# Attention with a separate maximum pass: chunks of 512 keys instead of 400 in that pass, and the last 66 keys of four query tiles in one chunk

## The chip, the cores and the metric

The kernel runs on one core of a Trainium2 chip. A core has a matrix engine (TensorE, PE in the profile; its weight loads are PEld), a vector engine (VectorE, DVE), a scalar engine (ScalarE, ACT), GpSimd (POOL), and a queue engine (SyncE, SP) that here only starts transfers. Each engine works through its own list of instructions in order and waits for the others by semaphores. The metric is the device time of one launch in microseconds (us). Matrix results go to PSUM, a small memory from which ACT and DVE read; a PSUM tile of this kernel is 128 partitions by two banks of 512 fp32 numbers.

## The reference

One layer of cross-attention and a feed-forward block over x (2048 rows of 256), with a context of 1601 keys of width 192, all in fp32:

```python
x = x + xattn(layernorm(x), ctx, mask, ...)
x = x + ffn(layernorm(x), k0, k1, k2, s0, s1, s2)

# xattn: 16 heads of 64
q, k, v = layer_norm(x) * g @ Wq, *split(ctx @ Wkv)
k, v = [null_k; k], [null_v; v]              # 1602 keys
attn = softmax(where(mask, q @ k.T / 8, -max))
out = layer_norm((attn @ v) @ Wout) * g_out
# ffn: three matrices of +1 and -1, relu between
```

The softmax needs a maximum over the 1602 keys for each query and head before the exponentials.

## The kernel before

The 16 heads are worked in 8 pairs p, the 2048 queries in 4 blocks b of 512: 32 units (p, b), written out in this order (`units`, L427), with the instructions of each engine in the order of the program (a manual schedule; no planner moves anything). A head of a pair lies on one half of the 128 partitions, so that matmuls for the two heads (j = 0, 1) use two halves of the array.

Scores are made twice. The exact pass (`exps`, L343) makes them in fp32 with the keys on the partitions, in 13 key tiles of 128 (the last has 66), two PSUM buffers in turn; for k < 2 a further matmul (L366) subtracts the maximum, and later tiles add the difference of the keys to what already lies in the buffer. ACT makes the exponentials (L368) into the tiles e, and POOL adds these up into acc (L556, L558), from which the denominator comes. The maximum pass (`max_chunk`, L310) makes the same scores in the rounded type fp32r, with the queries on the partitions: for each of the 4 query tiles t of a block the 1602 keys in 4 chunks (`CHUNKS`: 402, 400, 400, 400), each a pair of matmuls into a PSUM tile of its own and one DVE reduction (L321) over it. Unit u does the exact pass of its own block and, between the key tiles, the maximum pass of the next unit: 16 chunks behind 13 key tiles, two of them behind tiles 0, 4 and 8 (`extra`). `max_combined` (L323) takes the maximum over the four chunks.

After the key tiles PE runs the weighted sums (`weighted`, L375) for all 13 tiles, with the denominator of the unit before among them (`divided`, L390), then turns the maxima (`max_turned`, L328), projects the unit before's output (`project_out`), the queries of the unit after the next (`project_q`), and a part of the next pair's keys or values (`project_k`, `project_v`).

PSUM has two pools of two tiles: `spare` (the two score buffers, the weighted sum, the output projection) and `flex` (the chunks of the maximum pass, the denominator, the turned maxima, the other projections). A tile of a pool is free again when its reader is done. The last unit has no next one, and so no maximum pass.

Before the loop the first unit is prepared by hand (L478 to L518). There `CHUNKS` also sets how the context is loaded (L439) and how the first pair's keys are made (`first_keys`, L204), and the PSUM tiles come from both pools in turn (`slot`). Keys of the other pairs have a division of their own (L221). After the loop comes the feed-forward block (from L628), which the change doesn't touch.

Of the kernel before, what the change touches and what calls it, by code (L numbers as in the profile page):

```python
# [13 lines left out]
ALU = mybir.AluOpType  # L14
AX = mybir.AxisListType
# [5 lines left out]
KEYS = M + 1  # L21
CD = 192
HEADS, DH = 16, 64
# [3 lines left out]
NB = N // 512  # L27
KC = (KEYS + 127) // 128
KLAST = KEYS - 128 * (KC - 1)
CHUNKS = ((0, 402), (402, 400), (802, 400), (1202, 400))  # L30
EPS = 1e-5
MASKED = -3.0e38

# [2 lines left out]
def xattn_ffn(ctx, tc, x, ctxT, mask, g_norm, null_kv, wq, wkv, wout, g_out, k0, k1, k2, s0, s1, s2, out):  # L36
    nc = tc.nc
# [11 lines left out]
    def spare(name):  # L49
        return ps_s.tile([128, 2, 512], F32, tag="s", name=name)  # L50
# [92 lines left out]
    with ExitStack() as att:  # L143
# [40 lines left out]
        pairs, queries = {}, {}  # L184
# [19 lines left out]
        def first_keys(n, get):  # L204

            kT, _, kr = pairs[0]
            start, w = CHUNKS[n]
            keys = ds(start, w)
            ps = get(f"psk_0_{n}")
            nc.tensor.matmul(ps[:, 0, :w], weights[0][1][:, 0, :], ctx_a[:, keys], start=True, stop=False)  # L210
            nc.tensor.matmul(ps[:, 0, :w], weights[0][2][:, 0, :], ctx_b[:, keys], start=False, stop=True)

            nc.vector.tensor_tensor(kT[:, keys], ps[:, 0, :w], keep[:, keys], ALU.mult)
            nc.vector.scalar_tensor_tensor(kr[:, keys], drop[:, keys], nullk[:, 0:1], kT[:, keys], ALU.mult, ALU.add)
            if n == 0:
                nc.vector.tensor_copy(kT[:, 0:1], nullk)
# [25 lines left out]
        def keys_stepped(p):  # L242

            kT = pairs[p][0]
            for at in range(256 * ((KEYS - 1) // 256), 0, -256):
                w = min(256, KEYS - at)
                nc.gpsimd.tensor_tensor(kT[:, ds(at, w)], kT[:, ds(at, w)], kT[:, ds(at - 256, w)], ALU.subtract)  # L247

        def first_values(n, get):

            v = pairs[0][1]
            tiles = range(4 * n, min(4 * n + 4, KC))
            rows = 128 if n < 3 else KLAST
            ps = get(f"psv_0_{n}")
            for i, t in enumerate(tiles):
                keys = ds(128 * t, rows)
                out_t = ps[:rows, 0, ts(i, 128)]
                nc.tensor.matmul(out_t, ctx_a[:, keys], weights[0][1][:, 1, :], start=True, stop=False)
                nc.tensor.matmul(out_t, ctx_b[:, keys], weights[0][2][:, 1, :], start=False, stop=True)
            w = len(tiles)  # L260
            nc.scalar.copy(
                v[:rows, ds(4 * n, w), :], ps[:rows, 0, : 128 * w].rearrange("p (t d) -> p t d", d=128)
            )
            if n == 0:
                nc.vector.tensor_copy(v[0:1, 0, :], nullv)
# [42 lines left out]
        maxima, shifts = {}, {}  # L308

        def max_chunk(p, b, n, get=flex):  # L310
            t, c = divmod(n, 4)
            if n == 0:
                maxima[p, b] = wp.tile([128, 4, 2, 4], F32, tag="mx", name=f"mx_{p}_{b}")
            start, w = CHUNKS[c]
            ps = get(f"max_{p}_{b}_{n}")
            for j in range(2):
                rows = ts(j, DH)
                nc.tensor.matmul(  # L318
                    ps[:, j, :w], queries[p, b][1][rows, ts(t, 128)], pairs[p][2][rows, ds(start, w)], start=True, stop=True
                )  # L320
            nc.vector.tensor_reduce(maxima[p, b][:, t, :, c], ps[:, :, :w], AX.X, ALU.max)  # L321

        def max_combined(p, b):  # L323

            cols = mcol.rearrange("p (j c) -> p c j", j=2)[:, 0:4, :]
            nc.vector.tensor_reduce(cols, maxima[p, b], AX.X, ALU.max, negate=True)
# [13 lines left out]
        def rows_of(k):  # L340
            return 128 if k < KC - 1 else KLAST

        def exps(p, b, k, sT):  # L343

            kT, qT, mT = pairs[p][0], queries[p, b][0], shifts[p, b]  # L350
            n = rows_of(k)
            ps = sT[k % 2]
            for j in range(2):
                rows = ts(j, DH)
                nc.tensor.matmul(  # L355
                    ps[:n, j, :],
                    kT[rows, ds(128 * k, n)],
                    qT[rows, :],
                    start=k < 2,
                    stop=k >= 2,  # L360
                    skip_group_check=k >= 2,
                )
            if k < 2:
                for j in range(2):
                    rows = ts(j, DH)
                    nc.tensor.matmul(ps[:n, j, :], ones_r[rows, :n], mT[rows, :], start=False, stop=True)  # L366
            e = ep.tile([128, 2, 512], F32, tag="e", name=f"e_{p}_{b}_{k}")
            nc.scalar.activation(e[:n], ps[:n], AF.Exp, bias=maskb[:n, k : k + 1])  # L368
            return e
# [46 lines left out]
        def input_turned(b, get=flex):  # L416
            pt = get(f"xT_{b}")
            for j in range(4):
                for c in range(2):
                    nc.tensor.transpose(pt[:, c, ts(j, 128)], y_sb[:, 4 * b + j, ts(c, 128)], ident)  # L420
            nc.scalar.mul(xnT[:, b, 0, :], pt[:, 0, :], gn_sb[:, 0:1])
            if b == 1:
                nc.scalar.mul(xnT[:, b, 1, :], pt[:, 1, :], gn_sb[:, 1:2])
            else:
                nc.vector.tensor_scalar_mul(xnT[:, b, 1, :], pt[:, 1, :], gn_sb[:, 1:2])  # L425

        units = [(p, b) for p in range(NP) for b in range(NB)]  # L427
        extra = {0, 4, 8}

        begin = tc.manual_schedule()  # L430
        begin.__enter__()
# [1 line left out]
        def load_x(b):  # L433
            nc.sync.dma_start(out=x_sb[:, ts(b, 4), :], in_=x[ts(b, 512), :].rearrange("(c p) d -> p c d", p=128))

        load_pair(0)
        for b in range(1, NB):
            load_x(b)
        for n, (at, w) in enumerate(CHUNKS):  # L439
            skip = 1 if n == 0 else 0  # L440
# [45 lines left out]
        first_keys(1, slot)  # L486
        project_q(0, 0, slot)
        for t in range(4):
            max_chunk(0, 0, 4 * t, slot)
            if t == 1:  # L490
                first_keys(2, slot)
        for t in range(4):
            max_chunk(0, 0, 4 * t + 1, slot)
            if t == 1:
                first_keys(3, slot)
                keys_stepped(0)
# [6 lines left out]
        nc.vector.tensor_scalar(  # L503
            maskb[:KLAST, KC - 1 : KC], mcol_u8[:KLAST, KC - 1 : KC], -MASKED, MASKED, ALU.mult, ALU.add
        )
        for n in (2, 3):
            for t in range(4):
                max_chunk(0, 0, 4 * t + n, slot)
                if n == 2 or t == 3:
                    if t % 2 == 1:  # L510
                        first_values((0, 1)[t // 2] if n == 2 else 2, slot)
                if n == 3 and t == 1:
                    input_turned(1, slot)
        max_combined(0, 0)
        project_q(0, 1, slot)
        max_turned(0, 0)
# [3 lines left out]
        with tc.manual_schedule():  # L520
            for u, (p, b) in enumerate(units):
                nxt = units[u + 1] if u + 1 < len(units) else None
# [16 lines left out]
                    nc.gpsimd.tensor_tensor(y0, y0, gout_sb.unsqueeze(1).to_broadcast([128, 4, D]), ALU.mult)  # L539
                    nc.gpsimd.tensor_tensor(x0, x0, y0, ALU.add)  # L540

                es, n = [], 0
                acc = lp.tile([128, 2, 512], F32, tag="acc", name=f"acc_{p}_{b}")
                for k in range(KC):
                    if k == 0:

                        odd = spare(f"sT_{p}_{b}_1")
                        sT = [spare(f"sT_{p}_{b}_0"), odd]
                    es.append(exps(p, b, k, sT))
                    for _ in range(2 if k in extra else 1):  # L550
                        if nxt is not None:
                            max_chunk(*nxt, n)
                            n += 1
                    m = rows_of(k)
                    if k == 1:
                        nc.gpsimd.tensor_tensor(acc, es[0], es[1], ALU.add)  # L556
                    elif k > 1:
                        nc.gpsimd.tensor_tensor(acc[:m], acc[:m], es[k][:m], ALU.add)  # L558
# [199 lines left out]
```

## Time and profile before

| | |
|---|---|
| time, median of 3 runs | 1346.53 us (1346.41 to 1347.16) |
| the profiled execution | 1346.17 us, span 1344.1 us |
| granted TensorE clock | 0.994 |
| start, to the first scores of unit 0 | 48.5 us |
| 32 units | 48.5 to about 1155 us |
| feed-forward block | about 1155 us to the end |
| DVE reductions of the maximum pass (L321) | 512, 478.5 us busy, 987 ns each |
| PE matmuls of the maximum pass (L318) | 1024, 279.3 us busy |
| ACT exponentials (L368) | 416, 456.1 us busy, 1114 ns each |
| PE scores (L355) | 1664, 440.3 us busy |
| PE weighted sums (L375) | 1664, 369.5 us busy |

A group's "mean ns of one" is the time from its start to its end; instructions of one engine overlap, so that the distance from start to start, which the timeline gives, is shorter. An fp32 matmul appears as two passes, each with its own weight load, and a pair of heads as two rows of the same time. In the timeline the first column is the start, the second the length of the merged row, "xN" the instructions in it, and the brackets hold the idle time of the engine before it and who ended it.

### The profile page before, as it was taken

How to read it: one execution, taken by the hardware profiler on the slowest of the kernel's cores; microseconds unless marked ns; L12 is line 12 of the kernel's file. 1: busy time of each engine (PE TensorE's matmuls, PEld its weight loads, DVE VectorE, ACT ScalarE, POOL GpSimd, SP SyncE). 2: the span in 40 equal slices, each digit the busy share in tenths (PEclk: the TensorE clock that was granted, in tenths of full speed). 3: DMA queues.
4: the chain of work that ended last, by engine and by line, in shares of the span. 5: the costliest groups of instructions: out<-in, count | busy, mean ns of one | idle time of the engine just before them, and what ended most of it. 6: DMA issues, size and time to landing. Idle time of an engine off the chain costs nothing.

```text
span 1344.1 us, 16270 instructions
## 1 busy us (share of the span) xinstructions
PE 1304.6 (97%) x6528; PEld 654.8 (49%) x6528; DVE 845.8 (63%) x913; ACT 614.6 (46%) x676; POOL 1005.5 (75%) x508
## 2 busy tenths in 40 slices
PE   5989999999999999999999999999999999999998
PEld 2534444444444444444444444444444443688887
DVE  6777666666677566766666667666666784564431
ACT  1746444444444444445554555444444557421120
POOL 4468888898888888888888888888888999711100
PEclk9889999999999999999999999999999999999999
DMA  5000000000000000000000000000000010000000
GB/s 138 21 0 5 0 1 12 5 0 1 12 1 5 1 1 12 4 1 1 12 4 1 1 13 4 0 1 5 1 16 1 0 39 1 1 0 16 17 16 16
DMA packets 16092, 13.18 MB, mean 10 GB/s; under 512 B 2433, under 2 KB 15873, under 8 KB 16017
## 3 DMA queue, kind: packets, MB, share of 16 engines
q1 hardware_dynamic: 14640, 10.57, 2.8%
q10 hardware_dynamic: 896, 1.23, 0.3%
q8 instruction: 51, 0.84, 0.3%
q0 software_dynamic: 480, 0.34, 0.1%
q14 instruction: 25, 0.20, 0.0%
HBM read 10.04 MB, written 2.10 MB: 9 GB/s over the span
## 4 chain that ended last, share of the span: by engine, by line
PE 82%; ACT 8%; DVE 7%; issue 1%; DMA 1%; POOL 0%; SPq 0%; ACTq 0%; DVEq 0%
PE av L375 26%; PE sT L355 21%; PE ps L654 10%; PE max L318 6%; ACT e L368 6%; PE psq L199 4%; PE po L383 4%; DVE mx L321 4%; PE ps L677 2%; PE den L393 2%; PE psv L276 2%; PE psk L224 1%; DVE kr L236 1%; PE psv L288 1%; PE psk L229 1%
## 5 line engine op out<-in xcount | busy, mean ns | idle before, releaser
L558 POOL TENSOR_TENSOR acc<-acc,e 128x1024 f32<-128x1024 f32 (+1 forms) x352 | 849.4, 2413 | 27.6
L321 DVE TENSOR_REDUCE mx<-max 128x2 f32<-128x800 f32 (+1 forms) x512 | 478.5, 987 | 98.1 <-PE max L318 93.8
L368 ACT ACTIVATE e<-sT,maskb 128x1024 f32<-128x1024 f32 (+1 forms) x416 | 456.1, 1114 | 73.4 <-PE sT L355 44.7
L355 PE MATMUL sT<-qT,kT 64*128 64x512 f32 (+1 forms) x1664 | 440.3, 604 | 4.8 <-ACT e L368 1.3
L375 PE MATMUL av<-e,v 128*64 128x512 f32 (+1 forms) x1664 | 369.5, 594 | 0.8 <-ACT e L368 0.3
L318 PE MATMUL max<-kr,qr 64*128 64x400 f32 (+1 forms) x1024 | 279.3, 562 | 8.5 <-DVE mx L321 5.1
L375 PEld LDWEIGHTS av<-e,v 128*64 128x64 f32 (+1 forms) x1664 | 116.7, 137 | 237.8 <-issue 219.3
L318 PEld LDWEIGHTS max<-kr,qr 64*128 64x128 f32 x1024 | 97.6, 185 | 195.1 <-DVE mx L321 151.2
L355 PEld LDWEIGHTS sT<-qT,kT 64*128 64x128 f32 (+1 forms) x1664 | 139.7, 182 | 86.5 <-ACT e L368 75.5
L606 ACT COPY avs<-av 128x512 f32<-128x512 f32 x32 | 18.7, 585 | 324.0 <-PE av L375 324.0
L395 DVE RECIPROCAL aoT<-den 128x512 f32<-128x512 f32 x31 | 104.0, 3356 | 68.0 <-PE den L393 68.0
L556 POOL TENSOR_TENSOR acc<-e,e 128x1024 f32<-128x1024 f32 x32 | 77.5, 2421 | 86.2 <-ACT e L368 86.2
L333 DVE TENSOR_TENSOR mT<-mt,pick 128x512 fp32r<-128x512 f32 x32 | 22.1, 691 | 98.5 <-PE mt L331 98.5
L654 PE MATMUL ps<-h0hi,w 128*128 128x512 f32 x256 | 79.6, 392 | 0.0
L654 PE MATMUL ps<-h0lo,w 128*128 128x512 f32 x256 | 78.9, 389 | 0.0
L119 POOL TENSOR_TENSOR y_sb<-y_sb,gout_sb 128x256 f32<-128x256 f32 x12 | 9.3, 775 | 89.0 <-DVE y_sb L86 89.0
L200 ACT ACTIVATE qr<-psq 128x512 fp32r<-128x512 f32 x32 | 19.1, 597 | 100.4 <-PE psq L199 100.4
L199 PE MATMUL psq<-xnT,wq 128*128 128x512 f32 x128 | 62.1, 608 | 2.5 <-DVE xnT L425 2.5
L643 DVE SCALAR_TENSOR_TENSOR h1lo<-ps,h1hi 128x1024 fp32r<-128x1024 f32 x16 | 19.6, 1223 | 68.4 <-ACT h1hi L642 68.4
L383 PE MATMUL po<-wo,aoT 128*128 128x256 f32 x256 | 60.6, 380 | 0.0
L247 POOL TENSOR_TENSOR kT<-kT 128x256 f32<-128x256 f32 (+1 forms) x48 | 31.6, 659 | 38.3 <-DVE kr L236 22.1
L642 ACT ACTIVATE h1hi<-ps 128x1024 fp32r<-128x1024 f32 x16 | 16.4, 1025 | 94.6 <-PE ps L654 94.6
(147 smaller groups left out, 1025.6 us busy)
## 6 DMA issues: line engine op xcount, KB each, us to landing
x_sb<-in_x SPq DMA_DIRECT2D x4, 512.0 KB, 9.2
out_x<-o SPq DMA_DIRECT2D x8, 256.0 KB, 2.1
wa<-in_wkv SPq DMA_DIRECT2D x8, 128.0 KB, 2.8
wq<-in_wq SPq DMA_DIRECT2D x8, 128.0 KB, 2.2
wo<-in_wout SPq DMA_DIRECT2D x8, 128.0 KB, 2.1
xnT<-in_k SPq DMA_DIRECT2D x1, 1024.0 KB, 5.7
wb<-in_wkv SPq DMA_DIRECT2D x15, 64.0 KB, 2.4
ctx_a<-in_ctxT ACTq DMA_DIRECT2D x3, 200.0 KB, 6.8
```

Of the source, the lines that this page charges most:

```text
L199: nc.tensor.matmul(ps[:, 0, :], weights[p][0][:, c, :], xnT[:, b, c, :], start=c == 0, stop=c == 1)
L247: nc.gpsimd.tensor_tensor(kT[:, ds(at, w)], kT[:, ds(at, w)], kT[:, ds(at - 256, w)], ALU.subtract)
L318: nc.tensor.matmul(ps[:, j, :w], queries[p, b][1][rows, ts(t, 128)], pairs[p][2][rows, ds(start, w)], start=True, stop=True)
L321: nc.vector.tensor_reduce(maxima[p, b][:, t, :, c], ps[:, :, :w], AX.X, ALU.max)
L355: nc.tensor.matmul(ps[:n, j, :], kT[rows, ds(128 * k, n)], qT[rows, :], start=k < 2, stop=k >= 2, skip_group_check=k >= 2,)
L368: nc.scalar.activation(e[:n], ps[:n], AF.Exp, bias=maskb[:n, k : k + 1])
L375: nc.tensor.matmul(av[ts(j, DH), 0, :], v[:n, k, ts(j, DH)], e[:n, j, :], start=k == 0, stop=k == KC - 1)
L383: nc.tensor.matmul(pv[:, t, :], aoT[:, ts(t, 128)], weights[p][3], start=True, stop=True)
L395: nc.vector.reciprocal(aoT, ps)
L556: nc.gpsimd.tensor_tensor(acc, es[0], es[1], ALU.add)
L558: nc.gpsimd.tensor_tensor(acc[:m], acc[:m], es[k][:m], ALU.add)
L654: nc.tensor.matmul(ps[:, f, :], w(c)[:, ts(2 * g + f, 128)], parts[part][:, c, :], start=i == 0, stop=i == len(steps) - 1,)
```

## The change

The maximum pass divides the 1602 keys into three chunks of 512 and one of 66 (`CHUNKS`). For each query tile the three full chunks are a pair of matmuls and a reduction, as before: 12 of them. The 66 last keys of all four query tiles go into one PSUM tile, side by side (chunk number 12, `REST`): eight matmuls of 66 columns, and one reduction over 4 x 2 groups of 66. A unit then has 13 chunks, one behind each key tile, in the order 0, REST, 1, 2, ..., 11; `extra` is gone. In the preparation of the first unit the same 13 chunks stand in the order of the key chunks, with REST behind `input_turned(1)`, and the context is loaded and the first pair's keys are made in the new widths.

```diff
-CHUNKS = ((0, 402), (402, 400), (802, 400), (1202, 400))
+CHUNKS = ((0, 512), (512, 512), (1024, 512), (1536, KEYS - 1536))
+REST = 12
...
         def max_chunk(p, b, n, get=flex):
-            t, c = divmod(n, 4)
+            ps = get(f"max_{p}_{b}_{n}")
+            qr, kr = queries[p, b][1], pairs[p][2]
+            if n == REST:
+                start, w = CHUNKS[3]
+                for t in range(4):
+                    for j in range(2):
+                        rows = ts(j, DH)
+                        nc.tensor.matmul(
+                            ps[:, j, ts(t, w)], qr[rows, ts(t, 128)], kr[rows, ds(start, w)], start=True, stop=True
+                        )
+                nc.vector.tensor_reduce(
+                    maxima[p, b][:, :, :, 3].rearrange("p t j -> p j t"),
+                    ps[:, :, : 4 * w].rearrange("p j (t k) -> p j t k", k=w),
+                    AX.X,
+                    ALU.max,
+                )
+                return
+            t, c = divmod(n, 3)
             if n == 0:
                 maxima[p, b] = wp.tile([128, 4, 2, 4], F32, tag="mx", name=f"mx_{p}_{b}")
...
-        extra = {0, 4, 8}
+        order = (0, REST, *range(1, REST))
...
         for t in range(4):
-            max_chunk(0, 0, 4 * t, slot)
+            max_chunk(0, 0, 3 * t, slot)
...
-        for n in (2, 3):
-            for t in range(4):
-                max_chunk(0, 0, 4 * t + n, slot)
-                if n == 2 or t == 3:
-                    if t % 2 == 1:
-                        first_values((0, 1)[t // 2] if n == 2 else 2, slot)
-                if n == 3 and t == 1:
-                    input_turned(1, slot)
+        for t in range(4):
+            max_chunk(0, 0, 3 * t + 2, slot)
+            if t % 2 == 1:
+                first_values(t // 2, slot)
+        input_turned(1, slot)
+        max_chunk(0, 0, REST, slot)
+        first_values(2, slot)
         max_combined(0, 0)
...
                     es.append(exps(p, b, k, sT))
-                    for _ in range(2 if k in extra else 1):
-                        if nxt is not None:
-                            max_chunk(*nxt, n)
-                            n += 1
+                    if nxt is not None:
+                        max_chunk(*nxt, order[k])
```

## The prediction

> **What bounds the kernel now.** I read the page first: busy shares, then the chain that ended last.
>
> ```profile
> PE 1304.6 (97%) x6528; PEld 654.8 (49%) x6528; DVE 845.8 (63%) x913; ACT 614.6 (46%) x676; POOL 1005.5 (75%) x508
> ...
> PE 82%; ACT 8%; DVE 7%; issue 1%; DMA 1%; POOL 0%; SPq 0%; ACTq 0%; DVEq 0%
> PE av L375 26%; PE sT L355 21%; PE ps L654 10%; PE max L318 6%; ACT e L368 6%; PE psq L199 4%; PE po L383 4%; DVE mx L321 4%; PE ps L677 2%; PE den L393 2%; PE psv L276 2%; PE psk L224 1%; DVE kr L236 1%; PE psv L288 1%; PE psk L229 1%
> ```
>
> A busy PE is not a PE at its peak, and 97% hides two different stretches in each of the 32 units. Behind the scores, the weighted sums (L375) run back to back at 0.86 us per key tile: bound by PE. In the score stretch PE, ACT and DVE hand work round; the change acts there alone, and at the start. So I read the timeline of ACT for one such stretch with the maximum pass (unit 16) and for the only one without it (unit 31, no next unit):
>
> ```profile
> start us, us, engine line op out<-in xcount [idle before <-releaser]
> 614.33 1.12 ACT L368 ACTIVATE e<-sT,maskb 128x1024 f32<-128x1024 f32 x1 [0.42 <-PE sT L366]
> 615.78 4.66 ACT L368 ACTIVATE e<-sT,maskb 128x1024 f32<-128x1024 f32 x4 [0.34 <-PE sT L366]
> 620.77 2.25 ACT L368 ACTIVATE e<-sT,maskb 128x1024 f32<-128x1024 f32 x2 [0.33 <-PE sT L355]
> 623.18 2.25 ACT L368 ACTIVATE e<-sT,maskb 128x1024 f32<-128x1024 f32 x2 [0.15 <-PE sT L355]
> 625.76 4.61 ACT L368 ACTIVATE e<-sT,maskb 128x1024 f32<-128x1024 f32 x4 [0.33 <-PE sT L355]
> ...
> 1132.16 2.18 ACT L368 ACTIVATE e<-sT,maskb 128x1024 f32<-128x1024 f32 x2 [0.22 <-PE sT L355]
> 1134.56 2.18 ACT L368 ACTIVATE e<-sT,maskb 128x1024 f32<-128x1024 f32 x2 [0.22 <-PE sT L355]
> 1136.96 2.18 ACT L368 ACTIVATE e<-sT,maskb 128x1024 f32<-128x1024 f32 x2 [0.22 <-PE sT L355]
> ```
>
> Without a maximum pass two steps take 2.40 us (1132.16, 1134.56, 1136.96). That is a round trip: an exponential ends, 0.05 us later its PSUM buffer takes the scores two steps on, 1.24 us after that their exponential starts, and it lasts 1.11 us. In unit 16 the pairs with one chunk per step also take 2.40 (620.77 to 623.18): one chunk per step rides free. The pair that holds a step with two chunks takes 2.58 (623.18 to 625.76): the second chunk costs 0.18. PE shows why:
>
> ```profile
> 619.64 1.02 PE L355 MATMUL sT<-qT,kT 64*128 64x512 f32 x4
> 620.49 0.45 PE L318 MATMUL max<-kr,qr 64*128 64x400 f32 x2
> 620.78 1.02 PE L355 MATMUL sT<-qT,kT 64*128 64x512 f32 x4
> ```
>
> and DVE is nearly saturated, five reductions in 4.84 us, 0.90 from start to start:
>
> ```profile
> 618.30 4.84 DVE L321 TENSOR_REDUCE mx<-max 128x2 f32<-128x804 f32 x5 [0.16 <-PE max L318]
> ...
> 628.27 2.09 DVE L321 TENSOR_REDUCE mx<-max 128x2 f32<-128x800 f32 x2 [0.15 <-PE max L318]
> ```
>
> From first exponential to first weighted sum the timeline gives 15.04, 15.27, 15.25 and 15.11 us for blocks 0 to 3 (means), 15.17 over units 0 to 30, and 14.52 in unit 31. So all that the maximum pass costs in this stretch is 0.65 us a unit, 20.2 us in 31 units: the most the loop can give back.
>
> **The change, part by part.**
>
> *Ordinary chunks.* Twelve of 512 keys replace sixteen of 400, one behind each key tile. On PE the pair (two row halves at once) streams 400 columns in 0.167 us, by width 0.213 for 512; with the 0.018 seen between unlike matmuls, 0.23 a step. Scores take 0.857 (two passes 0.428 apart) and 0.105 of weight load when they had to wait: 1.19 in a step of 1.20. The longer chunk still fits, and its weights load behind the scores. The steps with two chunks (0, 4, 8) go: 0.18 each at 4 and 8, 0.13 at 0 (first to second exponential 1.45, to become 1.32). What is late next is again the round trip of 2.40.
>
> *DVE.* A reduction of 800 elements lasts 0.98 and the next starts after 0.898: 0.833 at 0.96 elements per ns and 0.065 more. By this 1024 elements start 1.13 apart and last 1.22, as the 1024-element PSUM reads of L388 do (1223 ns). Bounds 1.13 and 1.22; I take 1.13, from the same instruction. Either is hidden: a chunk's buffer is needed two steps (2.40) on, and 0.23 + 0.22 + 1.22 + 0.05 is 1.72. DVE ends about 1.4 us after the weighted sums begin (now 1.1); what waits there is the denominator's reciprocal, 3.7 us in. That cover would be gone only above 1.22 from start to start.
>
> *The shared chunk (REST).* Eight matmuls of 66 columns with eight weight loads, behind key tile 1, and a reduction of 528 elements (0.70 by the same arithmetic; nothing is queued tightly behind it). It waits for the buffer of the last projection, free by 613.9 in unit 16, before it is reached. No row has this shape. The nearest is the projection of values, alternating row halves with a new 128-column weight tile for each matmul:
>
> ```profile
> 714.40 1.95 PE L276 MATMUL psv<-wa,ctx_a 128*128 128x128 f32 x16
> 716.28 1.16 PE L288 MATMUL psv<-wb,ctx_b 64*128 64x128 f32 x16
> 717.27 1.03 PE L355 MATMUL sT<-qT,kT 64*128 64x512 f32 x4
> ```
>
> There the pairs start 0.112 apart with the loads hidden, so four pairs take 0.45 us. Lower bound: 66 of 400 columns of the present chunk, 4 x 0.028 = 0.11. Upper: loads not hidden and one after another, 8 x 0.183 (the duration of L318's load) = 1.46. I take 0.45, the same kind of work. In L288 every second load goes to the half whose matmul runs, and 0.112 has room for the load (0.105) or the matmul (128 of 512 columns of a pass of 0.428: 0.107), not for both in turn. The Trainium skill, "TensorE: Matmul & The Clock Gate", The mechanism, says that a weight load overlaps a running matmul only where their row groups differ. By that rule each half of REST would load and stream in turn, 4 x (0.105 + 0.028) = 0.53, and the sum would be 1333.0 instead of 1330.5; the trace speaks against it.
>
> From there: REST starts when tile 1's scores do their last column, 0.27 before the second exponential; tile 2's scores follow at 0.18 behind it, 0.857 + 0.27 later their exponential, at 1.31 instead of unit 31's 1.07. The odd tiles keep their beat (3 is due at 2.40, and 1.31 + 1.04 is less). The even ones keep the 0.24, and the last tile's scores and the last chunk push the weighted sums 0.11 past tile 11's exponential.
>
> *One unit.* 1.32 to the second exponential; 10.91 to tile 10's (1.31 + 4 x 2.40); its 1.11 + 0.05; weight load 0.105, scores 0.857, chunk 0.23: 14.59. The same arithmetic gives 15.01 and 15.22 for the present blocks 0 and 1, where 15.04 and 15.27 stand, so I add 0.05: 14.64. Saved: 31 x (15.17 - 14.64) = 16.4 us. Above 0.36, REST adds to each unit one for one.
>
> *Other engines.* POOL needs 29 us of additions a unit and 4.4 of key differences every fourth, 120 of 138.5 us; at 136.4 it still fits. At the end its additions run without a gap from unit 30 on, and the first h0lo is done 0.8 us before PE asks for it; about 0.35 of that is eaten. The SP and POOL queues issue as before.
>
> *The start.* The key projections and their loads take the new widths: the first two chunks of context are 256 KB for 200, landed about 10 us in where PE asks at 15.3, hidden. PE ran at half clock there (starts 0.667 apart), so psk of 512 instead of 400 is 0.56 late. Eight reductions before the statistics of block 1 cost 8 x 0.23 = 1.85 more, the 66-key step saves 0.75, the wider ones add 0.25: the statistics, and the ACT chain behind them to 38.5, come 1.95 later. After it two reductions and REST stand for six: the last ends at 44.4 for 45.7, but psv_2 waits for the copies of xT before it, which puts the first scores at about 48.9 for 48.5: +0.4. Ends: -1.3 (only the maximum counts) and +1.95 (all of ACT's delay).
>
> *Sum.* The profiled execution took 1346.17 (span 1344.1): 1346.17 - 16.4 + 0.4 = 1330.2. It stands 0.36 below the median of the runs shown, so 1330.5 for a median.
>
> **The rivals.**
> 1. *REST partly exposed*, 0.53 to 0.8 us: 14.72 to 14.99 a unit, 1333 to 1341. For it: pairs of L288 begin with a gap of 0.214.
> 2. *No change that shows.* The halves don't overlap, eight at the 0.112 of full-array L276: 0.90, 15.09 a unit, 1344.4. A reduction every 1.30 would do the same (15.2 by the recurrence). Against: both halves start within 0.01 us in L288 and L318. The Trainium skill, "TensorE: Matmul & The Clock Gate", Step-by-step, says that without hardware decoding the sequencer spends about 62 ns on a MATMUL. By that rule REST's eight need 0.50, and if loads counted the same 0.99: nothing gained. The trace does not bear it out: L288 issues two loads and two matmuls in 0.112.
> 3. *Slower.* REST stalls on its own weight loads, 1.46: 15.65 a unit, 31 x 0.48 = 14.9 more, 1361.8. It decides from 1.03 us on. For it: loads of 0.183 each, in one place (613.7) staggered by 0.12 between the halves. Against: L288, and the 0.105 that an exposed load really cost.
> 4. *Hidden entirely*, 0.3 or less: 14.52, the floor: 1326.7; inside the forecast's range.
>
> **How the numbers follow.** Forecast with rival 4 0.72 (1325 to 1335), rival 1 0.09, rival 2 0.06, rival 3 0.13. About 0.2% (2.7 us) is what a measurement of this kernel tells from no change: faster 0.81, same 0.06, slower 0.13. Low end: the floor and the start's -1.3, 1346.5 - 20.2 - 1.3 = 1325. High end: REST at 0.7 (14.89, -8.7) with the start's +1.95, 1340.
>
> **What would show it.** Pairs of exponentials 2.40 apart from tile 2 to 11 in every unit, none at 2.58; first exponential to first weighted sum 14.5 to 14.7; REST's four pairs 0.11 apart; reductions 1.13 apart; the first scores at 48 to 49.5. A gap over 1.7 between tiles 1 and 2, or ACT waiting behind DVE from tile 8 on, would make it wrong.

## The result and the profile after

The changed kernel takes 1330.39 us (median of 4 runs, 1330.09 to 1332.18); the kernel before took 1346.85 us in the same comparison (4 runs, 1346.41 to 1347.26). The ratio is 0.9881, with a 95% interval of 0.9864 to 0.9898: 1.2% faster. The profiled execution of the changed kernel took 1330.09 us, with a span of 1328.3 us for 1344.1 and a granted clock of 0.992 for 0.994.

The page of the changed kernel, its busy shares and its chain:

```profile
PE 1299.5 (98%) x6528; PEld 655.3 (49%) x6528; DVE 819.9 (62%) x817; ACT 618.9 (47%) x676; POOL 1003.4 (76%) x508
...
PE 92%; DVE 4%; ACT 2%; DMA 1%; issue 1%; POOL 0%; ACTq 0%; DVEq 0%
```

PE's busy time fell by 5.1 us (1304.6 to 1299.5), yet the span fell by 15.8. PE streams the same 1602 columns for each query tile in both. So most of the gain is not work that went away: it is waiting that went away. The chain says the same, with PE at 92% for 82%, ACT at 2% for 8% and DVE at 4% for 7%. The costliest groups of the two kernels say where. First the weight loads of the maximum pass before, then those and the reductions after; behind the bars stand the busy time and the mean, then the idle time of the engine ahead of the group and what ended most of it:

```profile
L318 PEld LDWEIGHTS max<-kr,qr 64*128 64x128 f32 x1024 | 97.6, 185 | 195.1 <-DVE mx L321 151.2
```

```profile
L338 DVE TENSOR_REDUCE mx<-max 128x2 f32<-128x1024 f32 x384 | 455.0, 1222 | 89.2 <-PE max L335 83.5
...
L335 PEld LDWEIGHTS max<-kr,qr 64*128 64x128 f32 x768 | 76.6, 188 | 94.0 <-DVE mx L338 46.9
```

Before, the loads stood 151.2 us behind a reduction that had not yet read the buffer; after, 46.9 us. The loads run ahead of the matmuls, so neither figure is lost time as it stands, but it tells whom to suspect. The timeline of ACT in unit 16 of the changed kernel (start, length of the merged row, number of exponentials, idle time before):

```profile
605.92 1.11 ACT L385 ACTIVATE e<-sT,maskb 128x1024 f32<-128x1024 f32 x1 [0.42 <-PE sT L383]
607.24 1.11 ACT L385 ACTIVATE e<-sT,maskb 128x1024 f32<-128x1024 f32 x1 [0.21 <-PE sT L383]
608.56 2.20 ACT L385 ACTIVATE e<-sT,maskb 128x1024 f32<-128x1024 f32 x2 [0.20 <-PE sT L372]
610.96 2.21 ACT L385 ACTIVATE e<-sT,maskb 128x1024 f32<-128x1024 f32 x2 [0.20 <-PE sT L372]
...
618.18 3.46 ACT L385 ACTIVATE e<-sT,maskb 128x1024 f32<-128x1024 f32 x3 [0.20 <-POOL acc L572]
```

From tile 2 on the pairs stand 2.40 us apart (608.56, 610.96, and so on to 618.18, which is four pairs or 9.62 us later), and none at 2.58: the beat of the unit without a maximum pass. Over the 31 units a pair takes 2.40 in the mean, and only units 4 and 12 hold a longer one (at most 2.68; see the end). Some rows name POOL as what the exponential waited for; the idle time is 0.20 there as in the rows that name PE, and POOL's additions of the unit before had ended at 604.0, so POOL doesn't hold ACT up. The first step lasts 1.32 us (1.45 before), and the second 1.32, which is REST's. From the first exponential to the first weighted sum the 31 units take 454.5 us in place of 470.3, 14.66 each for 15.17 (14.68, 14.66, 14.65 and 14.66 for blocks 0 to 3). That is 15.8 us, the whole difference of the spans. The first exponential of unit 0 comes at 49.89 for 49.92, and what lies between the score stretches and behind the loop is unchanged.

Now REST on PE, in the timeline of the same unit. An fp32 score matmul has two passes per half; the eight short matmuls of L319 are the 7 and the 1:

```profile
606.85 0.54 PE L319 MATMUL max<-kr,qr 64*128 64x66 f32 x7
607.22 0.67 PE L372 MATMUL sT<-qT,kT 64*128 64x512 f32 x1
607.23 0.27 PE L319 MATMUL max<-kr,qr 64*128 64x66 f32 x1
```

Unmerged, the starts on one half are 606.854, 606.884, 606.992 and 607.104, with the scores at 607.215; on the other half 606.980, 607.010, 607.119 and 607.231, with the scores at 607.343. (I tell the halves apart by their rhythm: the second row repeats the first 0.126 later.) The first matmul of a half takes 0.030, its weights having been loaded from 606.625 on while it waited; each of the others takes 0.11, and its load begins only 0.03 before it. From REST's first matmul to the next scores it is 0.36 us, and the scores' two passes then start 0.513 apart instead of 0.428, since the load of the first no longer hides: 0.45 in all. DVE, in its timeline of the same stretch:

```profile
607.55 0.71 DVE L322 TENSOR_REDUCE mx<-max 128x8 f32<-128x528 f32 x1 [0.23 <-PE max L319]
608.72 13.20 DVE L338 TENSOR_REDUCE mx<-max 128x2 f32<-128x1024 f32 x11 [0.46 <-PE max L335]
```

From 608.72 on eleven reductions follow in one row of 13.20 us, 1.20 on the average and 1.13 to 1.14 from start to start where the next is ready (the 1222 ns of the group overlap the next one). DVE is busy to the end of the stretch, and the beat of 2.40 shows no delay by it.

Last, the start, in PE's timeline and DVE's:

```profile
43.06 0.49 PE L259 MATMUL psv<-wa,ctx_a 128*128 128x128 f32 x2 [0.79 <-ACT xnT L440]
...
46.87 1.12 PE L372 MATMUL sT<-qT,kT 64*128 64x512 f32 x2
47.92 0.43 PE L259 MATMUL psv<-wa,ctx_a 128*66 128x128 f32 x2
48.50 0.69 PE L372 MATMUL sT<-qT,kT 64*128 64x512 f32 x1
```

```profile
46.97 0.69 DVE L350 TENSOR_TENSOR mT<-mt,pick 128x512 fp32r<-128x512 f32 x1 [3.07 <-PE mt L348]
```

The maxima are combined at 43.7 (45.7 before) and the first head's scores start at 46.87. But psv_3, which stands ahead of the second half of these scores, begins only at 47.92, 0.25 after DVE has read mt for mT (46.97 and 0.69), and the profile names that reading (mT L350) as what its load waited for; the scores go on at 48.50. The 1.2 us by which the turned maxima came sooner (mt at 46.66 for 47.88) are spent there: from mt to the first exponential it is 3.23 us, for 2.04 before.

### The profile page after: what moved, and what is told of

It reads as the page before. It is cut to its first block, busy times and chain, and to the rows that moved or that the text cites. A ratio compares the mean times of both kernels' runs of the same rounds, so it can differ in the third digit from the quotient of the medians.

```text
span 1328.3 us, 16173 instructions
## 1 busy us (share of the span) xinstructions
PE 1299.5 (98%) x6528; PEld 655.3 (49%) x6528; DVE 819.9 (62%) x817; ACT 618.9 (47%) x676; POOL 1003.4 (76%) x508
## 3 DMA queue, kind: packets, MB, share of 16 engines
q10 hardware_dynamic: 896, 1.23, 0.3%
## 4 chain that ended last, share of the span: by engine, by line
PE 92%; DVE 4%; ACT 2%; DMA 1%; issue 1%; POOL 0%; ACTq 0%; DVEq 0%
PE sT L372 29%; PE av L392 26%; PE ps L668 10%; PE max L335 6%; PE psq L200 4%; PE po L400 4%; PE ps L691 2%; PE den L410 2%; DVE mx L338 2%; PE psv L277 2%; PE psk L225 1%; PE sT L383 1%; PE psv L289 1%; PE psk L230 1%; PE max L319 1%
## 5 line engine op out<-in xcount | busy, mean ns | idle before, releaser
L338 DVE TENSOR_REDUCE mx<-max 128x2 f32<-128x1024 f32 x384 | 455.0, 1222 | 89.2 <-PE max L335 83.5
L372 PE MATMUL sT<-qT,kT 64*128 64x512 f32 (+1 forms) x1664 | 451.1, 613 | 1.2 <-ACT e L385 1.2
L335 PE MATMUL max<-kr,qr 64*128 64x512 f32 x768 | 293.3, 752 | 3.1 <-DVE mx L338 2.4
L372 PEld LDWEIGHTS sT<-qT,kT 64*128 64x128 f32 (+1 forms) x1664 | 130.2, 181 | 164.3 <-ACT e L385 155.3
L335 PEld LDWEIGHTS max<-kr,qr 64*128 64x128 f32 x768 | 76.6, 188 | 94.0 <-DVE mx L338 46.9
L350 DVE TENSOR_TENSOR mT<-mt,pick 128x512 fp32r<-128x512 f32 x32 | 22.1, 691 | 122.1 <-PE mt L348 122.0
L656 ACT ACTIVATE h1hi<-ps 128x1024 fp32r<-128x1024 f32 x16 | 16.4, 1026 | 94.6 <-PE ps L668 94.6
```

The costliest lines, as they stand in the source:

```text
L335: nc.tensor.matmul(ps[:, j, :w], qr[rows, ts(t, 128)], kr[rows, ds(start, w)], start=True, stop=True)
L372: nc.tensor.matmul(ps[:n, j, :], kT[rows, ds(128 * k, n)], qT[rows, :], start=k < 2, stop=k >= 2, skip_group_check=k >= 2,)
```

## The experiments

The first four experiments stand against 13 runs of the kernel before (median 1346.56 us), the other four against 7 (1347.27). I give the mean stretch from first exponential to first weighted sum as "the unit".

**REST three steps later.** Edit of the changed kernel:

```diff
-        order = (0, REST, *range(1, REST))
+        order = (0, 1, 2, 3, REST, *range(4, REST))
```

> The changed kernel with the shared chunk behind key tile 4 instead of tile 1. Theory of the round trip (two steps take 2.40 us whatever PE has to do in them, as long as it fits): behind an odd tile the shared chunk's 0.45 us of PE delays the even beat by about 0.1, which ends as a wait of the weighted sums for the last chunk; behind an even tile it delays the odd beat, whose last tile is not in front of the last chunk, and the delay is absorbed. First exponential to first weighted sum 14.5 to 14.55 instead of 14.66, and 3 to 4 us less in 31 units: 1326 to 1327.5. Rival (the time follows the total work on PE, which is the same wherever the chunk stands): no change, 1330.4.

Measured 1327.55 us (1326.74 to 1328.22), ratio 0.9861 (0.9844 to 0.9877). That interval overlaps the one of the changed kernel, so the time alone would not settle it; the timeline of ACT does (tiles 1 to 4 of unit 16, whose first exponential starts at 604.60):

```profile
605.92 2.22 ACT L385 ACTIVATE e<-sT,maskb 128x1024 f32<-128x1024 f32 x2 [0.21 <-PE sT L383]
608.33 2.22 ACT L385 ACTIVATE e<-sT,maskb 128x1024 f32<-128x1024 f32 x2 [0.19 <-PE sT L372]
```

The second to third exponential takes 1.10 us where it took 1.32, and no later gap is longer for having REST in it. The unit is 14.52 for 14.66, 4.3 us over the loop. The same eight matmuls with the same loads cost 0.14 a unit behind tile 1 and nothing behind tile 4. PE's time for them is the same in both places; what they cost depends on the slack of the step. The slack comes from the round trip. Behind tile 4, PE gets the next buffer only 1.16 after the exponential of tile 3 began (1.11 + 0.05). It is done with tile 4's scores 0.83 after that beginning (0.27 before the next exponential, 1.10 on), and 0.83 + 0.36 is 1.19. The 0.03 between the two don't show, because scores that wait for their buffer pay for their own load as well: from that load to the second pass it is 0.535 us at tile 4, which waits, and 0.538 at tile 5, behind REST. Behind tile 1 the first step is long (1.32, with the subtraction of the maximum in it), PE is done 1.05 after the first exponential began (1.32 - 0.27), and 1.05 + 0.36 is 1.41, against a buffer free at 1.16.

**REST's matmuls twice.** Edit of the changed kernel:

```diff
-                for t in range(4):
+                for t in (0, 1, 2, 3, 0, 1, 2, 3):
```

> The changed kernel with the eight matmuls of the shared chunk made twice (same results), which doubles its price on PE alone. Theory of the prediction (0.45 us for four pairs, and from there one for one): second to third exponential 1.31 to about 1.76, a unit 0.45 longer, 14 us in all: 1344.5, about the kernel before. Rival (the shared chunk hides in idle time of PE): under 0.1 a unit, at most 1333.5. Rival (loads not hidden): over 0.9 a unit, 1358 or more.

Measured 1345.31 us (10 runs, 1343.22 to 1348.13), ratio 0.9989 (0.9979 to 0.9998). ACT in unit 16:

```profile
616.28 1.12 ACT L385 ACTIVATE e<-sT,maskb 128x1024 f32<-128x1024 f32 x1 [0.20 <-PE sT L383]
618.04 2.21 ACT L385 ACTIVATE e<-sT,maskb 128x1024 f32<-128x1024 f32 x2 [0.65 <-PE sT L372]
```

The step grows from 1.32 to 1.76 (1.32 to 1.77 in the mean of the 31 units) and the unit from 14.66 to 15.11: 0.45 for four more pairs, both times. So the price of four pairs is 0.45 us where nothing hides it, and past the slack it goes into the unit one for one. It also gives back nearly all that the change gained: what the change would be worth had a pair cost twice as much.

**Half of each reduction, in the kernel before.** Edit:

```diff
-            nc.vector.tensor_reduce(maxima[p, b][:, t, :, c], ps[:, :, :w], AX.X, ALU.max)
+            nc.vector.tensor_reduce(maxima[p, b][:, t, :, c], ps[:, :, : w // 2], AX.X, ALU.max)
```

> The kernel before, all 16 chunks and all their matmuls, but each reduction reads only the first half of its columns (the maximum is then over half of the keys). It takes the time of DVE away and leaves PE's. Theory D (the second chunk of a step costs 0.18 because in the order of PE it waits for a buffer that DVE has not read yet; without that wait its 0.17 us fits into the idle time before the next scores): all pairs from tile 2 on at 2.40, a unit 14.6 to 14.7, 16 us less: 1330 to 1332, though nothing of the change is in it. Theory P (the second chunk costs its own PE time): the pairs with two chunks stay at 2.58 and the time at 1346 to 1347, less what the start gains.

Measured 1329.05 us (1326.74 to 1330.44), ratio 0.9869 (0.9854 to 0.9883). ACT in unit 16:

```profile
603.36 2.16 ACT L368 ACTIVATE e<-sT,maskb 128x1024 f32<-128x1024 f32 x2 [0.33 <-PE sT L366]
605.76 2.16 ACT L368 ACTIVATE e<-sT,maskb 128x1024 f32<-128x1024 f32 x2 [0.24 <-PE sT L355]
```

PE has all its sixteen chunks here, three steps still hold two of them, and yet the pairs are 2.40 apart throughout: the 2.58 is gone. So at tiles 4 and 8 it was not PE's time for the second chunk that cost 0.18; the chunk waited, in PE's own order, for a buffer that DVE had not read, and the scores stood behind it. In the kernel before, the weight loads of the second chunk behind tile 4 of unit 16 show the wait (the next scores start at 619.64):

```profile
619.35 0.19 PEld L318 LDWEIGHTS max<-kr,qr 64*128 64x128 f32 x2 [0.53 <-DVE mx L321]
```

At tile 0 the step keeps its 1.45, and there it is PE's time for the second chunk (with one chunk it is 1.27, in the next experiment). The unit is 14.67. The start is shorter too (first scores at 44.2 for 48.5), since its reductions were halved with the others; the 15.4 us of the loop are the part that answers the question.

**Thirteen chunks of 400, one in a step.** Edit of the kernel before:

```diff
-            nc.vector.tensor_reduce(cols, maxima[p, b], AX.X, ALU.max, negate=True)
+            nc.vector.tensor_reduce(cols, maxima[p, b][:, :, :, 0:1], AX.X, ALU.max, negate=True)
...
-        extra = {0, 4, 8}
+        extra = {}
```

> The kernel before with one chunk of 400 behind each key tile and the last three left out (a quarter of query tile 3's chunks is missing and only the first chunk of each query tile enters the maximum), in the loop alone. It is one chunk a step without the shared chunk and without the greater width. Theory of the round trip: a unit at the floor of 14.5 (14.42 by the recurrence, 14.52 in the unit without a maximum pass): 1325 to 1327. Rival (the time follows the work of DVE): three of 16 reductions gone, 2.7 us a unit, far below 1300.

Measured 1325.31 us (1323.93 to 1326.37), ratio 0.9842 (0.9827 to 0.9857). ACT in unit 16:

```profile
604.75 2.25 ACT L368 ACTIVATE e<-sT,maskb 128x1024 f32<-128x1024 f32 x2 [0.16 <-PE sT L366]
607.15 2.25 ACT L368 ACTIVATE e<-sT,maskb 128x1024 f32<-128x1024 f32 x2 [0.15 <-PE sT L355]
```

The first exponential stands at 603.48. The unit is 14.46. One ordinary chunk per step costs nothing that shows, and the first step is down to 1.27. That is 0.06 below unit 31, which the prediction had used as the floor. That unit's first step takes 1.34 us although no chunk is in it: its second scores start at 1125.94, behind DVE's reading of the unit before's output projection (L388, 1124.66 to 1125.89), which other units have done with sooner. So its 14.52 is not the least that a unit can take. The changed kernel is thus 0.20 a unit above what one chunk per step can reach: 0.14 is REST's place (the first experiment), and 0.05 to 0.06 the first step (1.32 for 1.27), about what 512 columns in its chunk take for 402 (by the prediction 0.213 us for 0.167 on PE).

**A short pad ahead of each reduction.** Edit of the changed kernel, in the loop (L338), where `scratch` is a tile of its own:

```diff
+            if p or b:
+                nc.vector.tensor_reduce(scratch[p, b][:, t, :, c], ps[:, :, :16], AX.X, ALU.max)
             nc.vector.tensor_reduce(maxima[p, b][:, t, :, c], ps[:, :, :w], AX.X, ALU.max)
```

> The changed kernel with a further small reduction on DVE (2 x 16 elements of the same chunk into a tile that nothing reads) ahead of each reduction of 512 keys in the loop: by the arithmetic of the reductions (0.065 us and 0.96 elements a ns) 0.10 us more from start to start, 1.23 in place of 1.13. Theory of the prediction (DVE is hidden up to about 1.22, then it becomes the bound slowly, over the twelve chunks): a unit unchanged to 0.1 longer, 1330 to 1333. Rival (the reductions stand on the path): 12 x 0.10 in 31 units, 37 us more, 1367.

Measured 1332.0 us (1329.74 to 1335.82), ratio 0.9892 (0.9873 to 0.9911), and the unit 14.67. The group of the pads on its page:

```profile
L340 DVE TENSOR_REDUCE sc<-max 128x2 f32<-128x32 f32 x372 | 68.4, 184 | 80.7 <-PE max L336 80.6
```

A pad lasts 184 ns but takes 0.098 from start to start; the reductions then start 1.229 apart, without a gap from the third chunk on. None of it shows in the unit. So DVE was indeed not the bound; it would become it somewhere above 1.23.

**A longer pad.** The same with `ps[:, :, :64]` (128 elements).

> The same with 2 x 64 elements: 0.20 us more from start to start, 1.33. Theory of the prediction: DVE falls behind by 0.13 a step and is late from about tile 10 on; a unit 15.1 in place of 14.66, 13 to 15 us more, 1343 to 1346. Rival (on the path from the start): 12 x 0.20 in 31 units, 74 us more. Rival (DVE never counts): no change.

Measured 1357.2 us (1356.81 to 1357.67), ratio 1.0078 (1.0061 to 1.0094), and the unit 15.43. DVE and then ACT in unit 16, tiles 8 and 9:

```profile
629.19 0.28 DVE L340 TENSOR_REDUCE sc<-max 128x2 f32<-128x128 f32 x1
629.39 1.22 DVE L341 TENSOR_REDUCE mx<-max 128x2 f32<-128x1024 f32 x1
630.52 0.28 DVE L340 TENSOR_REDUCE sc<-max 128x2 f32<-128x128 f32 x1
```

```profile
630.92 1.11 ACT L388 ACTIVATE e<-sT,maskb 128x1024 f32<-128x1024 f32 x1 [0.20 <-POOL acc L575]
632.21 1.11 ACT L388 ACTIVATE e<-sT,maskb 128x1024 f32<-128x1024 f32 x1 [0.17 <-PE sT L375]
```

Reductions come every 1.33 us (0.198 + 1.131), a tenth more than the step of 1.20, and DVE has become the bound: from tile 8 on each step takes 1.29 to 1.34 instead of 1.09 and 1.31 in turn, and a unit is 0.77 longer. So 1.23 from start to start still hides and 1.33 does not. The size was missed: I had expected 15.1, late from tile 10. A likely reason is that the pad stands ahead of the reduction, so that each buffer is also held 0.2 us longer, as much as DVE falls behind in one or two steps (0.13 each); that would make the delay show that much sooner. No run tests this by itself.

**REST later, and psv_3 ahead of the query projection.** The first experiment's edit, and in the start:

```diff
+        first_values(3, slot)
         project_q(0, 1, slot)
...
-        first_values(3, flex)
```

> The changed kernel with the shared chunk behind key tile 4 and, in the preparation of unit 0, the last values of the first pair (first_values(3)) ahead of the projection of the queries instead of behind the turned maxima, where they waited for DVE to read these (46.66 to 47.9 in the changed kernel) with the second half of the first scores behind them. If that wait sets the first exponential, it comes about 1 us sooner than in the changed kernel, at 48.8 for 49.9, and the time is 1.1 us below that with the shared chunk moved alone: about 1326.4. If the first exponential hangs on the maxima and not on this wait, no further gain.

Measured 1327.3 us (1326.84 to 1329.15), ratio 0.9857 (0.9842 to 0.9872). That can't be told from 1327.55, so what the wait of psv_3 costs the whole kernel is not shown. The trace shows the wait itself gone: from mt to the first exponential it is 1.61 us, where each of the six traces with the start of the changed kernel has 3.23. But PE ran at half clock from 44 to 50 us in this execution, mt came at 51.43 for 46.66, and the first exponential at 53.0. The units are the 14.52 of the first experiment. These two are the fastest versions that do the whole work, 1.4% faster than the kernel before.

**The same chunks, doubled as before.** Edit of the changed kernel: two chunks behind tiles 0, 4 and 8, one behind the others up to 9, none behind 10 to 12.

```diff
-        order = (0, REST, *range(1, REST))
+        order = iter((0, REST, *range(1, REST)) * len(units))
...
-                    if nxt is not None:
-                        max_chunk(*nxt, order[k])
+                    for _ in range(2 if k in (0, 4, 8) else 1 if k < 10 else 0):
+                        if nxt is not None:
+                            max_chunk(*nxt, next(order))
```

> The chunks of the change (twelve of 512 and the shared one, in the same order) in the places of the kernel before: two behind tiles 0, 4 and 8, one behind the others, none behind tiles 10 to 12. It undoes the one part of the change that the prediction rests on. Theory (in the order of PE the second chunk of a step waits for a buffer that DVE still reads, now for 1.22 us instead of 0.99): the double steps cost more than before, a unit 16.3 to 16.6, 35 to 45 us slower than the kernel before: 1382 to 1392. Rival (what counts is fewer and larger reductions): faster than before wherever the chunks stand, 1330 to 1340.

Measured 1384.17 us (one run), and the unit 16.50. ACT in unit 16:

```profile
634.57 4.68 ACT L385 ACTIVATE e<-sT,maskb 128x1024 f32<-128x1024 f32 x4 [0.65 <-PE sT L383]
639.89 4.67 ACT L385 ACTIVATE e<-sT,maskb 128x1024 f32<-128x1024 f32 x4 [0.65 <-PE sT L372]
645.57 2.25 ACT L385 ACTIVATE e<-sT,maskb 128x1024 f32<-128x1024 f32 x2 [1.00 <-POOL acc L573]
```

The first exponential stands at 632.80, so that the steps behind tiles 0, 4 and 8 take 1.77, 1.76 and 2.11 us. Fewer and larger reductions with the old distribution are 2.7% slower than the kernel before (1384.17 for 1347.27); the time is that of one run, but its trace has 41.1 us more in the 31 stretches alone. The smaller number of chunks gains nothing on its own: here it gains because 13 chunks can be dealt out one to a step.

## Why the prediction was right, step by step

The time came out (1330.5 us predicted, 1330.39 measured), a little better than its parts: the loop's gain was put 0.6 us too high and the start 0.4 us too late. That these cancel is luck.

- *The round trip of 2.40.* Right. The pairs stand 2.40 apart with 512-key chunks, and with 400-key ones (fourth experiment).
- *The doubled step at 0.18.* The price was right, the reading only half. "PE shows why" named the chunk on PE ahead of the scores (and its rows, 619.64 to 620.78, hold the single chunk behind tile 5; the second one behind tile 4 starts at 619.35), and DVE "nearly saturated". The third experiment shows that at tiles 4 and 8 the cost is the wait for DVE alone; at tile 0 it is PE's work.
- *REST at 0.45 us.* Right, twice (0.36 and 0.09 in the trace; 0.45 when doubled). Rivals 1, 2 and 3 asked for more than 0.53, 0.90 and 1.03, and fall. The rule of the Trainium skill, "TensorE: Matmul & The Clock Gate", The mechanism, that a load overlaps a running matmul only where row groups differ, would give 0.105 + 0.028 = 0.133 between matmuls of one half; the trace has 0.11. The time of about 62 ns for a MATMUL that the same page of the Trainium skill states for the sequencer without hardware decoding (Step-by-step) does not show either: two matmuls start in each 0.11.
- *REST's place.* Right: the even tiles keep the delay, and the end of the unit pays part of it (weighted sums 0.20 us behind the exponential of tile 11, predicted 0.11 + 0.05). Moving REST to where the round trip leaves room took 0.14 off a unit.
- *The unit.* 14.64 predicted, 14.66 measured; the loop gave 15.8 us for 16.4. The terms as printed add up to 14.58, not 14.59, which is 0.3 us of the forecast.
- *DVE hidden.* Right: 1.13 to 1.14 from start to start, and the last one ended 1.3 us after the weighted sums began (1.4 predicted). The border of 1.22 was a little low: 1.23 still hides, 1.33 does not.
- *The floor.* Wrong by 0.06: 14.52 was taken as the least a unit can take, from unit 31, and the fourth experiment reached 14.46. This end of the range would have been 1.9 us lower.
- *The start.* Wrong in size: +0.4 predicted, -0.03 measured. The term "psk 0.56 late" was priced at half clock throughout; its four passes started 0.85, 0.63 and 0.43 us apart, so that PE reached full clock among them, and the first reduction began at 20.96 for 20.83, 0.12 late. The statistics came 1.51 later instead of 1.95. The transposes of x took 1.09 us where they had taken 1.93 before. psv_2 did wait for the copies of xT, as predicted, but it began 0.9 us sooner than before all the same (43.06 for 43.97). What was not foreseen is psv_3 behind the reading of mt: in every trace with this start it is 3.23 us from mt to the first exponential, for 2.04 in every one with the start of the kernel before. That takes back the 1.2 us.

## What to carry to other kernels

When two buffers go round between PE and ACT, the round trip sets a beat, and side work on PE is free as long as each step's share fits the step's slack and its buffer is read in time; so deal it out evenly before making it cheaper. Work that is too large for one share belongs in the step with the most slack, which is found by comparing when PE is done with when it is allowed to go on: the same eight matmuls cost 0.14 us or nothing. And an engine that only fills gaps should be priced from start to start and against the beat, since the mean length of its instructions (1.22 us against a step of 1.20) would wrongly call it the bound.

## What the runs showed that I had not expected

The granted clock in the start differs between executions. The window of 40 to 48 us, changed kernel first and the seventh experiment second; PEclk is the third column from the end:

```profile
40.00:48.00 8.00, 7.21 (x44) 4.89 (x44) 3.98 (x6) 4.08 (x8) 0.00 (x0) 0.96 0.01 2
```

```profile
40.00:48.00 8.00, 5.77 (x38) 5.30 (x38) 3.28 (x5) 3.77 (x7) 0.00 (x0) 0.73 0.01 2
```

The kernel before has 0.79 there. The first exponentials then came at 49.9 and 53.0 us. A difference of a microsecond in the start can't be read from one trace of each kernel; the loop repeats better, with 14.52 us a unit in the first experiment and in the seventh.

Matmuls of 66 columns in fp32r with new weights follow each other on one half of the array after 0.11 us, against 0.030 where the weights had been loaded already. The weight load sets the pace (where it stood exposed ahead of scores in the kernel before, their passes were 0.533 apart for 0.428, 0.105 more), and the columns add next to nothing to it.

One thing stays open: unit 12 is longer than unit 16, of the same block, in both kernels (14.94 for 14.66; before, 15.21 for 15.00), and in both it is the gap between the second and third exponential that is 0.28 longer. In unit 4 of the changed kernel it is a later pair, with 2.68. No run here tells why.
